# A two-layer attention and feed-forward kernel: first stack by groups of heads, empty products at the start, and row products with 72 columns of weights

## The chip, the cores and the metric

The kernel runs on one core of a Trainium2 chip. A core has a matrix engine (TensorE, here PE, whose weight loads are listed apart as PEld), a vector engine (VectorE, DVE), a scalar engine (ScalarE, ACT), a general engine (GpSimd, POOL), a queue engine (SyncE, SP) and sixteen DMA engines. Each engine works through its own instructions in the order in which they were written; between engines semaphores order the work. The metric is the time of one execution in microseconds on the device, as the median of several runs.

## The reference

The input is x of 8 batches x 512 tokens x 256 channels and a context of 8 x 512 x 128. Four blocks follow each other, each added to its input after a layer norm:

```python
x = x + L0_xattn(layernorm(x), ctx)   # causal self attention + cross attention, 16 heads of 16
x = x + L0_ffn(layernorm(x))          # quantised per token, 256 -> 1024 -> 256, gelu
x = x + L1_xattn(layernorm(x), ctx, ctx)  # cross attention, 16 heads of 16
x = x + L1_ffn(layernorm(x))          # quantised per tensor, 256 -> 1024 -> 256, gelu
# an attention: softmax(q @ k.T / 4) @ v for each head, then an output projection
# (for the self attention, keys after the query are masked)
```

All attention products are computed near single precision: a query or key is split into a high part and the rest, and the product of the two is taken as three terms.

## The kernel before

**Units, preps and groups.** An attention of one batch is a unit: S (causal self attention), C (cross attention of the first layer), X (cross attention of the second). There are 24 units. Each has 16 heads; a prep `n` covers the 8 heads of half a unit, and a group `G` covers 4 heads, as two pairs with one head in partitions 0 to 63 and one in 64 to 127. So unit 0 has preps 0 and 1, and groups 0 and 1 (of prep 0), 2 and 3 (of prep 1).

**What a prep does.** `ln_job` normalises x and turns it on TensorE into channels x tokens (`xlt`). `prep_job(n)` (line 550) multiplies it with the query and key weights, ScalarE adds the bias, and the result is split in a high and a low part (for preps 0 and 1 on VectorE, for all others on GpSimd). `stack_job(n)` (line 597) then copies by DMA, SBUF to SBUF, the parts into `qk_t`: 48 rows per head, three for each of 16 channels (high, low, high against high, high, low). It is six transfers of 256 KB, all issued from SP. Row 48 and 49 of a head carry the row maximum in two parts; the key side has ones there, written once by `init_job` (line 1361).

**What a group does.** `max_one` (line 668) multiplies queries with keys for a pair, both heads side by side in 64 rows of the array each, with 128 columns of weights; VectorE takes the negative maximum of each row into `mx`. For S units, mask products come first. `rows_job(n)` (line 706) waits for both groups of a prep, splits the maxima in two parts on GpSimd (`mhl`) and turns them into rows on TensorE: for each of 4 query tiles, and each half of 64 partitions, one product with 16 columns of weights and 64 moving columns. Two evacuations and two small transfers put the rows into `qk_t`. `exp_one` (line 756) then multiplies keys with queries over 50 rows, so that the maximum is already subtracted, and ScalarE takes the exponential into `p`. `av_part` (line 804) multiplies `p` with the values, four heads at a time in strips of 32 columns.

**What sets the order.** The whole program is laid out in Python before it runs. `Plan` (line 77) keeps a clock for each engine with modelled costs; `until(key)` lets a job wait until that event has a planned time. Each job is a generator, with a priority. The main loop (line 1452) picks, on TensorE's planned clock, the next maximum step, exponential step or value step, or lets a job run. Instructions land in each engine's queue in that order, and at run time each queue is in order. Thus SP issues transfers in planned order: one that waits for its data holds all behind it. `at["stack", G]` is the planned landing of the stack; V weights (`weights_job`), `init_job` and the next inputs (`inputs_jobs`) wait for `("stack", 0)`.

**The start.** SP issues x of batch 0 (512 KB, line 330), the first query and key weights (line 337), eight small transfers of biases (line 369), eight of identity and mask (line 374), and then the second halves of query and key weights (line 442). VectorE takes the batch-norm statistics and also reorders the columns of those four weights by small copies (line 449).

**Drains of the array.** The plan counts `SWITCH` when TensorE goes between products in 32-column strips over 128 rows ("cols") and products over 64 rows ("rows"); row products count as "rows", with `ROW_COLS` = 600 columns a block.

Of the kernel before, what the change touches and what calls it, by code (L numbers as in the profile page):

```python
# [17 lines left out]
P = 128  # L18
NT = T // P
# [57 lines left out]
class Plan:  # L77
# [43 lines left out]
    def dma(self, kb, *deps, dims=2, rate=195):  # L121
        t = self.run("sp", 0.33 if dims == 2 else 0.65, *deps)
        self.clock["dma"] = max(self.clock["dma"], t + 0.95) + kb / rate
        return self.clock["dma"] + 0.35
# [100 lines left out]
GQ, AHEAD = 4, 3  # L225
LINGER = 0.2
ROW_COLS = 600
DVE_HANDICAP = 0.8


# [56 lines left out]
def build(tc, A, out):  # L287
# [39 lines left out]


    first_x = tile("xa", [P, NT, C], F32, "xa_s0")
    nc.sync.dma_start(first_x, A["x"][0])  # L330
    at["x0"] = dma(512)
    heapq.heappop(plan.rings["xa"])
    first_raw = {}
    for i, nm in enumerate(("Sq", "Sk")):
# [16 lines left out]
    one = const.tile([P, 1], F32, name="one")  # L351
    nc.vector.memset(one, 1.0)
    ones_sq = one.broadcast_to([P, P])

    ident2 = const.tile([P, 2, P], BF16, name="ident2")
    mask2 = const.tile([P, 2, P], BF16, name="mask2")
# [75 lines left out]
    def weights_job():  # L432
        order = [(nm, u) for nm in ("Sq", "Sk", "Cq", "Ck", "Xq", "Xk") for u in range(2)]
        order[:4] = [("Sq", 0), ("Sk", 0), ("Sq", 1), ("Sk", 1)]
        for n, (nm, u) in enumerate(order):
            nk = WT[nm].shape[2]
            if n < 2:
                raw, t = first_raw[nm], at["raw", nm]
            else:
                yield from take("oc")  # L440
                raw = tile("oc", [P, T], F32, f"raw_{nm}{u}")
                nc.sync.dma_start(raw[:, : nk * P], WSRC[f"{nm}{u}"])
                t = dma(64 * nk)
            yield t + LAT
            for k in range(nk):
                for h in range(2):
                    full = raw[:, k * P : (k + 1) * P].rearrange("p (g c d h) -> p h c d g", g=2, c=2, h=2)
                    dst = WT[nm][:, u, k].rearrange("p (c d g h) -> p h c d g", c=2, g=2, h=2)
                    (nc.vector if n < 4 else nc.gpsimd).tensor_copy(dst[:, h], full[:, h])
                    t = plan.run("dve" if n < 4 else "pool", 0.2)  # L450
            give("oc", t)
            at["w", nm, u] = t
            if n == 3:
                yield from until(("stack", 0))
                for v in ("Vs", "Vc", "Vx", "Wp", "Wo"):
                    nc.sync.dma_start(WT[v].rearrange("p k m -> p (k m)"), WSRC[v])
                    at["w", v] = dma(256)
# [11 lines left out]
    def stats(x, nm):  # L469

        st = wp.tile([P, NT, 6], F32, tag="bnst", name=f"st_{nm}", bufs=3)
        mv = wp.tile([P, NT, 2], F32, tag="bnmv", name=f"mv_{nm}", bufs=3)
        r = wp.tile([P, NT], F32, tag="rstd", name=f"r_{nm}", bufs=3)
        neg = wp.tile([P, NT], F32, tag="nmean", name=f"nm_{nm}", bufs=3)
        for t in range(NT):
            nc.vector.bn_stats(st[:, t, :], x[:, t, :])
            op("dve", C)
            yield plan.now + 0.4
        for t in range(NT):
            nc.vector.bn_aggr(mv[:, t, :], st[:, t, :])  # L480
        te = plan.run("dve", 0.4)
        nc.gpsimd.tensor_scalar(r, mv[:, :, 1], LN_EPS, 0.0, ALU.add, ALU.add)
        nc.gpsimd.tensor_tensor(r, r, mhalf, ALU.pow)
        nc.gpsimd.tensor_scalar(neg, mv[:, :, 0], -1.0, 0.0, ALU.mult, ALU.add)
        te = plan.run("pool", 1.3, te)
        return mv[:, :, 1], neg, r, te
# [7 lines left out]
    def ln_job(key, src, nm, n_uses):  # L494

        if key[0] == "X":
            yield from until(("x3", key[1]))
        if key == ("S", 0):
            x = first_x
            yield at["x0"] + LAT  # L500
        else:
            yield from take("xa")
            x = tile("xa", [P, NT, C], F32, f"xa_{nm}")
            nc.sync.dma_start(x, src())
            yield dma(512) + LAT
        var, neg, r, te = yield from stats(x, nm)
        yield te
        for t in range(NT):
            if key == ("S", 0):
                at["first"] = nc.vector.tensor_scalar(  # L510
                    x[:, t, :], x[:, t, :], neg[:, t : t + 1], r[:, t : t + 1], ALU.add, ALU.mult
                ).ins.name
                te = op("dve2", C, te)
            else:
                te = normalise(x[:, t, :], x[:, t, :], neg, r, t)
        yield from take("xlt")
        xlt[key] = tile("xlt", [P, 2, T], F32, f"xlt_{nm}")
        uses[key] = [n_uses, 0.0]
        for k in range(2):
            yield pe_next(te)  # L520
            ps, pb = yield from gen_bank()
            for t in range(NT):
                wide(ps[:, t * P : (t + 1) * P], x[:, t, k * P : (k + 1) * P], ident)
            tm = plan.pe(4 * T, "cols")
            tm = evacuate(xlt[key][:, k, :], ps, T, tm)
            give_bank(pb, tm)
        give("xa", tm)
        at[key] = tm
# [21 lines left out]
    def prep_job(n):  # L550
# [26 lines left out]
        for i, (hi, lo) in enumerate(((0, 1), (3, 2))):  # L577
            wname, which = KIND[kind][i]
            key, ring = src_key(kind, b, which)
            yield from until(key, ("w", wname, u))  # L580
            xs = xlt[key]
            nk = xs.shape[1]
            ps, pb = yield from gen_bank()
            for k in range(nk):
                yield pe_next()
                wide(ps, WT[wname][:, u, k], xs[:, k, :], k == 0, k == nk - 1)
                tm = plan.pe(4 * T, "cols")
            used(key, ring, tm)
            ready.append((wname, ps, pb, tm, hi, lo))
            if n >= 2 or i == 1:  # L590
                for r in ready:
                    th = yield from split(*r)
                ready = []
# [3 lines left out]
    def stack_job(n):  # L597

        yield from until(("qkt", n))
        tf, tl = qkt_t.pop(n)  # L600
        if n >= NQK:
            yield from until(("exp", 2 * (n - NQK) + 1))
        dst = qk_t[n % NQK].bitcast(F32)
        for r, parts in enumerate((slice(0, 4, 3), slice(1, 4, 2), slice(0, 3, 2))):
            yield (at["qkt", n] if r < 2 else tl[1]) + LAT
            for c in range(2):
                nc.sync.dma_start(
                    dst[64 * c + r : 64 * c + 48 : 3].rearrange("p g w n -> p (g w n)"),
                    tf[64 * c : 64 * c + 64, parts, :],
                )  # L610
                t = dma(256, dims=3)
        at["stack", 2 * n] = at["stack", 2 * n + 1] = t
        give("qkt", t)

    VW = {"S": ("Vs", "S"), "C": ("Vc", "K"), "X": ("Vx", "K")}
# [87 lines left out]
        if s + 1 == len(MAX_STEPS) or MAX_STEPS[s + 1][0] != G:  # L703
            at["max", G] = t

    def rows_job(n):

        yield from until(("max", 2 * n), ("max", 2 * n + 1))
        m = mx_t.pop(n).rearrange("p c g t -> p t c g")
        hl = wp.tile([P, NT, 2, 2, 4], F32R, tag="mhl", name=f"mhl{n}", bufs=1)  # L710
        copy_ts(hl[:, :, :, 0], m)
        nc.gpsimd.tensor_tensor(hl[:, :, :, 1], m, hl[:, :, :, 0].bitcast(F32), ALU.subtract)
        t = plan.run("pool", 0.5)
        give("mx", t)
        yield pe_next(t)
        row = wp.tile([16, T], F32R, tag="mrow", name=f"mrow{n}", bufs=1)

        while (t := plan.bank_at("gn", 2)) is None:
            yield plan.now + 0.2
# [3 lines left out]
        for qt in range(NT):  # L723
            for h, i in enumerate(got):
                half = slice(64 * h, 64 * h + 64)
                nc.tensor.matmul(
                    banks[i][:16, qt * P :][:, half], hl[half, qt].rearrange("p c a g -> p (c a g)"), ident_r[half, half],
                    start=True, stop=True,
                )
        tm = plan.pe(ROW_COLS, "rows")  # L730
        t = 0.0
        for h, i in enumerate(got):
            dst, src = (
                x.rearrange("p (t n) -> p t n", t=NT)[:, :, 64 * h : 64 * h + 64] for x in (row, banks[i][:16])
            )
            te = evacuate(dst, src, T // 2, tm)
            give_bank(i, te)
            t = max(t, te)
        yield t + LAT
        for c in range(2):  # L740
            nc.sync.dma_start(
                qk_t[n % NQK].bitcast(F32)[64 * c + 48 : 64 * c + 50, :, 0], row.bitcast(F32)[8 * c : 8 * c + 8]
            )
            t = dma(16, dims=3)
        at["rows", 2 * n] = at["rows", 2 * n + 1] = t

    p_t, p_at, p_slots, av_t, scr_o = {}, {}, {}, {}, {}

# [610 lines left out]


    def init_job():
        yield from until(("stack", 0))
        yield from take("ev")
        ones = tile("ev", [4, T], F32, "ones_rows")

# [31 lines left out]
            if kind == "X":  # L1397
                yield from ln_job(("X", b), lambda b=b: x3_d[b], f"x{b}", 2)

    plan.start(series(rows_job(n) for n in range(2 * NU)), 0)  # L1400
    plan.start(series(evac_job(G) for G in range(NG - 2)), 0)
    plan.start(weights_job(), 0)
    plan.start(inputs_jobs(), 1)
# [370 lines left out]
```

## Time and profile before

| what | value |
|---|---|
| median of 3 runs | 1462.89 us (1462.37 to 1465.43) |
| the profiled execution | 1460.25 us, its span 1458.4 us |
| granted TensorE clock, mean | 0.971 |
| TensorE busy | 1374.8 us (94% of the span) |
| VectorE busy | 1142.0 us (78%) |
| ScalarE busy | 1035.5 us (71%) |
| GpSimd busy | 681.6 us (47%) |
| DMA queue of SP | 204.73 MB, 58.0% of 16 engines |
| row products, 64 rows x 16 columns, 64 moving | 384, in 48 blocks of 8 |

Page lines give busy time, share of the span and number of instructions of each engine, and then the span in 40 equal slices (36.5 us each): each digit is the busy share in tenths, and for PEclk the granted clock of TensorE in tenths of full speed. A timeline line has the start, the length, engine, source line, operation, output <- inputs, shapes and how many were merged; in brackets the idle time of the engine before it and what ended it. Nearly all operations carry the line of a helper (241 or 259), so tiles tell them apart: `pair<-qk` is a score product for maxima, `bank<-qk` one for exponentials, `bank<-ident_r,mhl` a row product, `bank<-p,v` a value product, `qk<-qkt` a stack transfer, `qk<-mrow` a transfer of rows. A busy PE counts from a product's start to its modelled end; consecutive products overlap, so steps between starts are read for rates.

### The profile page before, as it was taken

The page shows a single profiled execution, that of the slowest core. Times are in us where ns is not written, and L with a number is a line of the kernel's source. Part 1 is how long each engine was busy: PE and PEld are TensorE (multiplying, and loading weights), DVE is VectorE, ACT ScalarE, POOL GpSimd, SP SyncE. Part 2 cuts the span into 40 slices and gives each one's busy share as a digit, 9 for nine tenths or more (in the row PEclk, how much of TensorE's full clock was granted, in tenths as well). Part 3 has the DMA queues.
Part 4 walks back from the last instruction along what each step waited for, and adds up shares of the span by engine and source line. Part 5 has one row for each costly group of instructions (what it writes and reads, how often), then busy time and mean ns, then how long its engine had stood idle before and what let it go on. Part 6 is the DMA issues. An engine that isn't in the chain of part 4 may idle for free. (4 is left out here: it accounts for less than half of the span.)

```text
span 1458.4 us, 36089 instructions
## 1 busy us (share of the span) xinstructions
PE 1374.8 (94%) x14400; PEld 597.5 (41%) x14400; DVE 1142.0 (78%) x1591; ACT 1035.5 (71%) x1904; POOL 681.6 (47%) x1025
## 2 busy tenths in 40 slices
PE   4999999999999999999999999999999998999978
PEld 2443444444444444434344433443333333333527
DVE  4678588697788886898777996689899888766397
ACT  1456767677768867767677777668778795777587
POOL 1463355465455465464653552654455541524332
PEclk8899999999999999999899999999999999999899
DMA  6593565667576755665457655556647657373343
GB/s 126 152 216 76 133 139 125 142 138 182 132 161 150 161 129 141 156 161 126 105 126 155 163 126 132 142 120 160 163 105 169 155 149 196 105 176 110 117 142 116
DMA packets 155612, 207.03 MB, mean 142 GB/s; under 512 B 71940, under 2 KB 74244, under 8 KB 154932
## 3 DMA queue, kind: packets, MB, share of 16 engines
q1 hardware_dynamic: 155444, 204.73, 58.0%
q8 instruction: 113, 1.85, 0.5%
q14 instruction: 55, 0.45, 0.1%
HBM read 68.15 MB, written 47.43 MB: 79 GB/s over the span
## 5 line engine op out<-in xcount | busy, mean ns | idle before, releaser
L241 DVE TENSOR_REDUCE mx<-pair 128x2 f32<-128x1024 f32 (+3 forms) x768 | 808.9, 1086 | 210.7 <-PE pair L259 194.6
L241 ACT ACTIVATE p<-bank 128x512 f32<-128x512 f32 (+1 forms) x1408 | 712.0, 587 | 232.7 <-PE bank L259 224.8
L259 PE MATMUL bank<-p,v 128*32 128x512 f32 (+3 forms) x3072 | 371.7, 563 | 2.9 <-DVE mrow L241 1.3
L259 PE MATMUL bank<-qk 50*128 50x512 f32 (+3 forms) x1536 | 337.6, 433 | 16.2 <-ACT p L241 8.0
L259 PE MATMUL pair<-qk 48*128 48x512 f32 (+3 forms) x1536 | 325.5, 438 | 25.7 <-DVE mx L241 11.8
L259 PEld LDWEIGHTS bank<-qk 50*128 50x128 f32 x1536 | 159.6, 190 | 215.7 <-ACT p L241 142.9
L259 PEld LDWEIGHTS pair<-qk 48*128 48x128 f32 x1536 | 148.0, 191 | 171.5 <-DVE mx L241 83.4
L384 POOL TENSOR_SCALAR qkt<-qkt 128x512 fp32r<-128x512 f32 x92 | 57.1, 621 | 164.1 <-ACT qkt L241 157.5
L241 ACT ACTIVATE qkt<-bank,qk_bias 128x512 f32<-128x512 f32 x96 | 66.6, 693 | 81.0 <-PE bank L259 65.4
L409 POOL TENSOR_TENSOR qkt<-qkt 128x512 fp32r<-128x512 f32 x92 | 118.8, 1291 | 7.7
L259 PEld LDWEIGHTS bank<-p,v 128*32 128x32 f32 x3072 | 70.9, 109 | 114.6 <-issue 85.9
L384 POOL TENSOR_SCALAR mhl<-mx 128x32 fp32r<-128x32 f32 x48 | 11.8, 245 | 171.3 <-DVE mx L241 164.8
L883 POOL TENSOR_TENSOR yt<-oc,rb 128x512 f32<-128x512 f32 x31 | 39.8, 1283 | 73.3 <-DMA rb<-scrz 50.9
L259 PE MATMUL pair<-mask,ident 64*128 64x128 bf16 (+2 forms) x768 | 58.0, 226 | 6.9 <-DVE mx L241 4.7
L259 PE MATMUL bank<-ident,mask 64*128 64x64 bf16 (+1 forms) x768 | 52.7, 206 | 3.7 <-ACT p L241 1.2
L259 PEld LDWEIGHTS <-ident 64*128 64x128 bf16 x768 | 26.1, 97 | 71.0 <-issue 52.8
L259 PEld LDWEIGHTS <-mask 64*128 64x128 bf16 x768 | 25.8, 96 | 69.3 <-issue 61.0
L241 ACT COPY v<-bank 128x512 f32<-128x512 f32 x44 | 26.2, 596 | 39.4 <-PE bank L259 39.1
L241 ACT COPY ev<-bank 128x512 f32<-128x512 f32 x56 | 33.5, 598 | 17.9 <-PE bank L259 17.9
L241 DVE SCALAR_TENSOR_TENSOR h<-bank,so,bc_l_b 128x512 f32<-128x512 f32 x64 | 45.3, 741 | 0.9 <-PE bank L259 0.7
L241 ACT ACT_TABLE_LOAD x34 | 43.6, 1283 | 1.9 <-PEq L1762 0.7
L1189 POOL TENSOR_SCALAR h<-h,sh 128x1024 f32<-128x1024 f32 x32 | 36.0, 1125 | 17.7 <-DVE sh L241 15.2
(230 smaller groups left out, 1686.4 us busy)
## 6 DMA issues: line engine op xcount, KB each, us to landing
qk<-qkt SPq DMA_DIRECT2D x288, 256.0 KB
scro<-ev SPq DMA_DIRECT2D x94, 256.0 KB
oc<-scro SPq DMA_DIRECT2D x47, 256.0 KB
rb<-scrz SPq DMA_DIRECT2D x47, 256.0 KB
x_d<-xb SPq DMA_DIRECT2D x15, 512.0 KB
xa_s<-in_x SPq DMA_DIRECT2D x8, 512.0 KB
xb<-in_x SPq DMA_DIRECT2D x8, 512.0 KB
xr<-x_d SPq DMA_DIRECT2D x16, 256.0 KB
```

The costliest lines, as they stand in the source:

```text
L241: r = f(*args, **kw)
L259: r = self.eng.matmul(out, *args, **kw)
L384: nc.gpsimd.tensor_scalar(dst, src, 1.0, 0.0, ALU.mult, ALU.add)
L409: nc.gpsimd.tensor_tensor(dst, full, high.bitcast(F32), ALU.subtract)
L883: nc.gpsimd.tensor_tensor(y, o, rb, ALU.mult)
L1189: nc.gpsimd.tensor_scalar(ht, ht, s[:, t - t0 : t - t0 + 1], MAGIC, ALU.mult, ALU.add)
```

## The change

- x of batch 0 is loaded by two transfers of 256 KB.
- The column copies of the first query and key weights go to ScalarE; those of the second stay on VectorE.
- `keep_warm(n)` issues products of 128 rows, 128 columns and 512 moving columns of zeros into a bank pair that nothing reads: 8 at the start, 2 behind each of the four batch-norm statistics, 3 after them, and 16 behind prep 1's last projection.
- The stack of prep 0 is done by groups of heads: group 0's two pairs first, then group 1's, by 24 transfers of 64 KB, alternately from SP and ScalarE's queue. `at["stack", 0]` and `at["stack", 1]` are now two events; V weights and the rows of ones wait for the second, the next inputs for the first.
- For prep 0 a row job runs for each group by itself; all other preps are as before.
- A row product takes 72 columns of weights (`WIDE`): its 16 (or 8) columns and whatever lies behind them in a tile that is cleared once. The additional output rows are not read.

```diff
+WIDE = 72
...
-    nc.sync.dma_start(first_x, A["x"][0])
-    at["x0"] = dma(512)
+    for t in range(0, NT, 2):
+        nc.sync.dma_start(first_x[:, t : t + 2], A["x"][0][:, t : t + 2])
+        at["x0", t] = dma(256)
...
+    zero_b = zero.bitcast(BF16)[:, 0:1]
+
+    def keep_warm(n, behind=None):
+
+        for _ in range(n):
+            r = nc.tensor.matmul(
+                pairs[3][:, 0], zero_b.broadcast_to([P, P]), zero_b.broadcast_to([P, T]), start=True, stop=True
+            )
+            if behind is not None:
+                tc.add_manual_dep(r.ins, behind.ins.name, SYNC, reason="warm")
+                behind = None
+
+    keep_warm(8)
...
-                    (nc.vector if n < 4 else nc.gpsimd).tensor_copy(dst[:, h], full[:, h])
-                    t = plan.run("dve" if n < 4 else "pool", 0.2)
+                    if n < 2:
+                        nc.scalar.copy(dst[:, h], full[:, h])
+                    else:
+                        (nc.vector if n < 4 else nc.gpsimd).tensor_copy(dst[:, h], full[:, h])
+                    t = plan.run("act" if n < 2 else "dve" if n < 4 else "pool", 0.2)
...
             if n == 3:
-                yield from until(("stack", 0))
+                yield from until(("stack", 1))
...
-            nc.vector.bn_stats(st[:, t, :], x[:, t, :])
+            r_st = nc.vector.bn_stats(st[:, t, :], x[:, t, :])
+            if nm == "s0":
+                keep_warm(2, r_st)
...
+        if nm == "s0":
+            keep_warm(3, r_st)
...
-            yield at["x0"] + LAT
+            yield at["x0", 0] + LAT
...
+            if (n, i) == (1, 1):
+                keep_warm(16)
...
+        rows = (slice(0, 4, 3), slice(1, 4, 2), slice(0, 3, 2))
+
+        for g in range(2 if n == 0 else 0):
+            for r, parts in enumerate(rows):
+                yield (at["qkt", n] if r < 2 else tl[1]) + LAT
+                for pair in (2 * g, 2 * g + 1):
+                    for c, q in enumerate((nc.sync, nc.scalar)):
+                        q.dma_start(
+                            dst[64 * c + r : 64 * c + 48 : 3, pair], tf[64 * c + pair : 64 * c + 64 : 4, parts, :]
+                        )
+                    plan.run("act", 0.65)
+                    t = dma(128, dims=3)
+            at["stack", g] = t
+        for r, parts in enumerate(rows if n else ()):
...
-        at["stack", 2 * n] = at["stack", 2 * n + 1] = t
+        if n:
+            at["stack", 2 * n] = at["stack", 2 * n + 1] = t
...
+    hl_t = wp.tile([P, 48 + WIDE], F32R, name="mhl")
+    nc.gpsimd.memset(hl_t.bitcast(F32), 0.0)
+
+    def rows_job(n, g0, ng):
+
+        yield from until(*(("max", 2 * n + g) for g in range(g0, g0 + ng)))
+        last = g0 + ng == 2
+        ps = slice(2 * g0, 2 * (g0 + ng))
+        m = mx_t[n].rearrange("p c g t -> p t c g")[:, :, :, ps]
+        k = 8 * ng
+        hl = hl_t[:, : NT * k].rearrange("p (t c a g) -> p t c a g", t=NT, c=2, a=2)
...
-                    banks[i][:16, qt * P :][:, half], hl[half, qt].rearrange("p c a g -> p (c a g)"), ident_r[half, half],
+                    banks[i][:WIDE, qt * P :][:, half], hl_t[half, qt * k : qt * k + WIDE], ident_r[half, half],
...
-        at["rows", 2 * n] = at["rows", 2 * n + 1] = t
+        for g in range(g0, g0 + ng):
+            at["rows", 2 * n + g] = t
...
     def init_job():
-        yield from until(("stack", 0))
+        yield from until(("stack", 1))
...
-    plan.start(series(rows_job(n) for n in range(2 * NU)), 0)
+    rows = [(0, 0, 1), (0, 1, 1)] + [(n, 0, 2) for n in range(1, 2 * NU)]
+    plan.start(series(rows_job(*r) for r in rows), 0)
```

## The prediction

> **What bounds the kernel now.** I read the page first: engines, then slices.
>
> ```profile
> PE 1374.8 (94%) x14400; PEld 597.5 (41%) x14400; DVE 1142.0 (78%) x1591; ACT 1035.5 (71%) x1904; POOL 681.6 (47%) x1025
> ...
> PE   4999999999999999999999999999999998999978
> ...
> PEclk8899999999999999999899999999999999999899
> ```
>
> TensorE bounds everything but the first slice (36 us, PE 4 tenths) and the tail. So the change has two prices: what the start gives back, and what a longer row product adds in the middle. The tail's chain (27 us of DVE gmax, 26 us of output products) isn't touched.
>
> Next the timeline of the first 60 us (start, length, instruction, idle before it and its releaser).
>
> ```profile
> 12.40 0.53 SPq L442 DMA_DIRECT2D raw_Sq<-in_wa  x1
> ...
> 14.74 0.54 DVE L241 COPY w_Sq<-raw_Sq 128x64 f32<-128x64 f32 x4 [4.66 <-DMA raw_Sq<-in_wa]
> ...
> 15.63 0.42 DVE L241 CAST qkt<-qkt 128x512 fp32r<-128x512 f32 x1
> ...
> 17.49 9.00 SPq L607 DMA_DIRECT2D qk<-qkt  x12
> ...
> 18.03 0.69 ACT L241 ACTIVATE qkt<-bank,qk_bias 128x512 f32<-128x512 f32 x1 [1.03 <-PE bank L259]
> ...
> 27.27 0.47 PE L259 MATMUL pair<-qk 48*128 48x128 f32 x1 [7.31 <-DMA qk<-qkt]
> ...
> 45.31 0.24 POOL L384 TENSOR_SCALAR mhl<-mx 128x32 fp32r<-128x32 f32 x1 [31.84 <-DVE mx L241]
> ...
> 56.89 2.06 ACT L241 ACTIVATE p<-bank 128x512 f32<-128x512 f32 x4 [2.75 <-PE bank L259]
> ```
>
> The stack (twelve transfers of 256 KB for preps 0 and 1) is issued from 17.49; scores begin at 27.27, when the first six have landed. Both groups' maxima end at 45.3 (POOL takes them up), and the first exponential runs at 56.89. The same stretch by windows (length, busy PE, PEld, DVE, ACT, POOL, granted clock, DMA share, GB/s):
>
> ```profile
> 20.00:27.00 7.00, 0.00 (x0) 0.00 (x0) 1.12 (x2) 0.43 (x1) 0.00 (x0) 0.70 1.08 192
> 27.00:34.00 7.00, 4.81 (x36) 3.79 (x36) 3.98 (x7) 0.00 (x0) 0.00 (x0) 0.50 1.08 190
> 34.00:44.00 10.00, 9.35 (x82) 4.89 (x82) 7.17 (x10) 0.42 (x1) 0.00 (x0) 0.54 0.89 268
> ...
> 120.00:1340.00 1220.00, 1175.42 (x12696) 492.20 (x12692) 985.57 (x1348) 898.56 (x1706) 592.25 (x883) 0.98 0.60 142
> ```
>
> To be seen: the stack runs at 190 GB/s with the DMA full, PE idles 7 us, then works at half clock until 43; in the middle PE is busy 96%.
>
> Last, a row product between scores (PE timeline, near 1222 us), and the loads of a 128-column score pair:
>
> ```profile
> 1221.84 0.49 PE L259 MATMUL pair<-qk 48*128 48x512 f32 x2
> 1222.17 0.29 PE L259 MATMUL bank<-ident_r,mhl 64*16 64x64 f32 x8
> 1222.32 0.50 PE L259 MATMUL pair<-qk 48*128 48x512 f32 x2
> ```
>
> ```profile
> 45.53 0.31 PEld L259 LDWEIGHTS pair<-qk 48*128 48x128 f32 x4
> ```
>
> **The front end (x halves, copies on ACT, warm-up).** x landed at 4.37. In halves, the first about 1 us earlier; without the eight weight copies (2 x 0.52) between its instructions DVE ends the statistics at about 5.5, not 6.9, and normalising starts near 7.3, not 8.7. Nineteen empty products of 512 columns, at 0.215 us warm (the tail's 512-column products step by that) or 0.43 at half clock, take 4 to 8 us of a PE with nothing to do before 9.16; transposes that took 3.59 should come near twice 1.07, the warm pair at 65 and 67 us. So the first projections end some 2.5 us earlier. I cost this at **nothing**, because of a queue: SP issues without a pause to 13.4, and the second pair of raw weights is issued at 12.40, behind sixteen small transfers of 0.6 each. The extra x half moves it to 12.84. Its copies stay on DVE, and in the order written out they precede the splits (planned about 9 us, the splits after 12). So DVE splits from 15.63 + 0.44 = 16.07, then by rows 0.45 + 0.69 + 0.43: first stack issue at about **17.65**, 0.15 later than before. What the cover is worth if gone: 2.5 us.
>
> **The stack in groups.** Prep 0 becomes 24 transfers of 64 KB, half from ACT. Group 0 is 12: six per queue at about 0.7 (SP's twelve took 9.0) end at 21.9; its 786 KB at 190 GB/s need 4.1, so issue and data agree on landing near **23.4**, against 27.27: -3.9. Group 1 lands near 27.5. The Trainium skill speaks against the second queue ("DMA: Bandwidth & Descriptors", Issuing engines are not separate DMA queues): transfers from several engines run on the same DMA engines, and only issue time is saved. The row says when that matters: at 256 KB the rate bound it (1.38 us of data per 0.75 of issue); at 64 KB the data take 0.34 and one queue's issue 0.7. From one queue group 0 would land at 28, by two at 23.4; I take the row.
>
> What stands behind ACT's twelve issues: prep 1's two evacuations, 18.03 and 19.75 before. They wait until 17.65 + 12 x 0.67 = 25.7; DVE's splits follow, and prep 1's stack is issued near 28. Context and next x (768 KB; the plan releases them at group 0's landing) now go ahead of it. Its 1.57 MB land near 39 instead of 35. Needed then? Before, the second prep's maxima began only at 44.9.
>
> **Array warm at the scores.** Sixteen empty products follow prep 1's last projection, which the second raw weights still hold to about 19.6: 3.4 us, to 23.0, just before the stack lands. They delay nothing unless the stack comes earlier. Then DVE sets the pace: the sixteen maxima of both groups are 3.08 + 6.35 + 2.00 + 1.23 = 12.7 us of DVE, stretched to 17.9 at half clock. From 23.4 they end near 37, not 45.3: -8. Group 0's rows are ready near 31. First exponentials still need the rows of ones (issued 37.4 to 41.6 before, now behind prep 1's stack) and their own small transfer: about 46, not 56.9: -10.9. Meanwhile V, the next transposes and the next query projection fill PE. Prep 2 moves too: its key weights were issued at 49.71 behind a row transfer on which SP had stood 4.7 us. So between 8 and 11; since maxima lead by less, I take **-9**. Ends: 0 if something late takes it back, -13 if prep 2 comes 10 us earlier as well.
>
> **The row products.** 48 blocks of 4 x 2, 16 columns wide, become 49 (the extra one in the DVE-bound start, with two POOL operations, two evacuations, two 8 KB transfers: hidden). The two halves run side by side; pairs step by 0.03 us, 64 columns streamed. A 72-column load is longer than that. The row: a 128-column pair of the same type steps 0.31 - 0.19 = 0.12. The skill ("TensorE: Matmul & The Clock Gate", LDWEIGHTS) has columns / 1.2 in ns: 107 at 128, where the row agrees, and an estimate of 60 at 72, where no row is. Three steps: +0.09. After a product in 32-column strips the first load isn't hidden: +0.05 more. I counted 21 blocks behind scores or masks, 27 behind others: 21 x 0.09 + 27 x 0.14 = **5.7 us of PE**.
>
> And what is saved? The skill ("TensorEngine Tiling (Array Packing)", Key Properties) says that a change of tiling mode drains the array; 16 columns are another mode than 128. Of the blocks' 96 borders 41 are to scores or masks. The drain that the trace shows, between 128-row and 64-row products, is 0.095 (512-column strip products step 0.427, to a score 0.522). By the rule 41 x 0.095 = 3.9 saved, net +1.8. The row: a score at 1221.84, a load of 0.11 and 0.21 of streaming end at 1222.16; the product starts at 1222.17. After it a score follows in 0.15, and at 941.82 within 0.03 of the last product. There is no drain to save; I take the row. Some added time falls into PE's waits (4% of the middle), so of 5.7 I count **+3.5**; ends -1 and +5.7.
>
> **Sum.** -9 + 3.5 = -5.5. The profiled execution took 1460.25 (span 1458.4, 1.85 around it), 2.6 below the median of 1462.89; on the median: **1457.4**. A planner orders everything from one clock, so a moved start shuffles all later queues; I allow 3 us either way.
>
> **Rivals.**
> - Slower: *prep 1's stack late behind ACT's queue.* For: twelve issues precede two evacuations, and two loads go ahead of its six transfers. Each microsecond past 39 is taken from the start; at 45 to 46 nothing is left, since maxima of prep 1 began at 44.9. An issue on ACT of 1.0, as SP's longest here (1.01), adds 4; loads of V weights (1.3 MB) slipped ahead add 3.5 to 7. Then only the row loads remain: 1462.9 + 3.5 = **1466.4**. Against: 6 us of slack.
> - *The division does pay*: a cost of 16 columns that single starts don't show, or loads hidden. Rows cost 0 or -1: **1453**.
> - *The array isn't warm*: score products with gaps may not hold the clock; at half clock the maxima take 17.9 again. Only -3.9 remains, plus 3.5: **1462.5**. For: 27 to 43 stayed at half clock though PE worked.
>
> **How the numbers follow.** As worked out 0.45 (1454 to 1461), division pays 0.17, late stack 0.28, array cold 0.10. A measurement of this kernel tells about 0.2% (2.9 us) from no change. Faster: the first two, 0.62; same: mainly the cold array, 0.10; slower: 0.28. The range leaves out the outer part of the first and last: 1450 to 1468; the likeliest's own is 1454 to 1461.
>
> **What would show it.** First stack issue at 17.5 to 17.8 (at 15: the front end counted after all); first score at 23 to 24; clock full from about 20; maxima of group 1 done near 37; first exponential near 46; ACT evacuating prep 1 near 26; prep 1's maxima by 40. In the middle: 72-column pairs stepping 0.06, not 0.03, and the same 0.02 at borders to scores. I am wrong if first exponentials stay near 56, or if the blocks take no longer than before.

## The result and the profile after

The changed kernel takes 1479.26 us, median of 4 runs (1476.72 to 1482.22), against 1462.63 us of the kernel before in the same set (4 runs). The ratio is 1.0109, 95% interval 1.0077 to 1.014. The forecast was 1457.4, range 1450 to 1468. It is **slower by 16.6 us** where 5.5 us of gain were expected. The profiled execution took 1476.72 (span 1474.9).

The page of the kernel after: engines, then the row of TensorE's busy tenths and the row of its granted clock.

```profile
PE 1387.3 (94%) x14436; PEld 605.6 (41%) x14443; DVE 1139.3 (77%) x1583; ACT 1040.2 (71%) x1914; POOL 679.5 (46%) x1028
...
PE   7999999999999999999999999999999999999978
...
PEclk9989999999999999999989999989999999899999
```

TensorE is busy 12.5 us more than the 1374.8 shown of before, and its first slice has gone from 4 tenths to 7. Some of that is the empty products. The timeline of the first 62 us (start, length, instruction, the idle before it and what ended that):

```profile
13.39 0.53 SPq L457 DMA_DIRECT2D raw_Sq<-in_wa  x1
...
15.75 0.53 DVE L242 COPY w_Sq<-raw_Sq 128x64 f32<-128x64 f32 x4 [7.44 <-DMA raw_Sq<-in_wa]
...
16.64 0.43 DVE L242 CAST qkt<-qkt 128x512 fp32r<-128x512 f32 x1
...
18.16 7.74 SPq L635 DMA_DIRECT2D qk<-qkt  x12
18.16 8.07 ACTq L242 DMA_DIRECT2D qk<-qkt  x12
...
23.55 0.88 PE L260 MATMUL pair<-qk 48*128 48x128 f32 x4
...
26.28 1.26 ACT L242 ACTIVATE qkt<-bank,qk_bias 128x512 f32<-128x512 f32 x2 [12.37 <-PE pair L260]
...
34.22 5.05 SPq L644 DMA_DIRECT2D qk<-qkt  x6
...
43.77 0.21 POOL L399 TENSOR_SCALAR mhl<-mx 128x16 fp32r<-128x16 f32 x1
...
47.86 4.03 ACT L242 ACTIVATE p<-bank 128x512 f32<-128x512 f32 x8 [0.59 <-PE bank L260]
```

This is nearly the start that was forecast. DVE waits for the second raw weights (13.39), the stack of prep 0 is issued at 18.16 on both queues, the first score runs at 23.55, where it was 27.27, and the first exponential at 47.86, where it was 56.89: 9 us earlier. Two steps are late: prep 1's stack is issued at 34.22, and GpSimd takes up group 1's maxima at 43.77 (DVE ends them at 42.76). By windows (length, busy PE, PEld, DVE, ACT, POOL, granted clock, DMA share, GB/s):

```profile
20.00:27.00 7.00, 5.41 (x37) 2.86 (x36) 2.49 (x5) 0.72 (x2) 0.00 (x0) 1.00 0.56 201
27.00:34.00 7.00, 4.05 (x34) 2.90 (x34) 6.50 (x11) 0.54 (x1) 0.44 (x2) 0.63 0.87 298
34.00:44.00 10.00, 10.00 (x146) 4.81 (x148) 6.81 (x14) 2.82 (x6) 6.20 (x16) 0.92 0.89 170
120.00:1340.00 1220.00, 1169.56 (x12546) 493.11 (x12543) 970.73 (x1331) 888.44 (x1684) 575.52 (x857) 0.97 0.61 140
```

The clock is full when the scores start, falls to 0.63 between 27 and 34, and is 0.92 in the next ten microseconds. In the middle TensorE is busy 1169.56 of 1220 us, where it was 1175.42. So the start was won, and yet the end is late. The windows of the first 130 us say where the head start went. The kernel after:

```profile
0.00:60.00 60.00, 50.12 (x616) 26.16 (x617) 32.25 (x76) 22.38 (x50) 17.59 (x47) 0.94 0.57 165
60.00:130.00 70.00, 61.48 (x578) 24.61 (x578) 52.43 (x68) 32.03 (x64) 41.74 (x62) 0.88 0.58 129
```

and the kernel before:

```profile
0.00:60.00 60.00, 39.33 (x434) 22.00 (x436) 35.77 (x83) 11.07 (x19) 13.72 (x34) 0.80 0.58 140
60.00:130.00 70.00, 68.31 (x728) 28.47 (x726) 50.67 (x71) 41.72 (x88) 44.14 (x71) 0.95 0.62 150
```

In the first 60 us the changed kernel starts 616 products, 34 of them empty, against 434. From 60 to 130 us it starts 578 against 728. After 130 us both stand at almost the same count (1160 useful ones against 1162): a head start of some 150 products is gone, and the clock of the second window is 0.88 where it was 0.95. The timeline of that stretch in the kernel after:

```profile
48.22 2.00 SPq L1112 DMA_DIRECT2D bc_l_b<-in_l_b  x2
...
50.27 0.43 SPq L1282 DMA_DIRECT2D l0w1f<-in_l_w  x1
...
51.13 0.33 SPq L457 DMA_DIRECT2D raw_Ck<-in_wb  x1
...
59.56 0.46 POOL L467 COPY w_Ck<-raw_Ck 128x64 f32<-128x64 f32 x2 [1.53 <-DMA raw_Ck<-in_wb]
```

```profile
65.33 0.62 POOL L399 TENSOR_SCALAR qkt<-qkt 128x512 fp32r<-128x512 f32 x1
...
65.97 5.41 SPq L644 DMA_DIRECT2D qk<-qkt  x6
...
76.44 0.79 PE L260 MATMUL pair<-qk 48*128 48x512 f32 x1 [5.14 <-DMA qk<-qkt]
```

Prep 2's first key weights leave SP at 51.13, behind two bias rows and the 1 MB of the FFN's first weights. GpSimd's copy waits for them to land and starts at 59.56, 8.4 us after the issue. ACT has evacuated the projection at 61.98, but GpSimd first works off what stands ahead in its queue, the normalising of the next input and two copies of weights; it splits prep 2 at 65.33, and SP issues its stack at 65.97. TensorE, which has by then used up all that preps 0 and 1 gave, stands 5.14 us for it. From 73.1 to 83.4 the granted clock is half. In the kernel before, split and stack were at the same times, and prep 2's first score 2.7 us later:

```profile
42.57 0.43 SPq L1232 DMA_DIRECT2D l0w1f<-in_l_w  x1
...
49.71 12.23 SPq L442 DMA_DIRECT2D raw_Ck<-in_wb  x2
...
61.53 0.48 POOL L449 COPY w_Ck<-raw_Ck 128x64 f32<-128x64 f32 x2
...
65.49 0.62 POOL L384 TENSOR_SCALAR qkt<-qkt 128x512 fp32r<-128x512 f32 x1 [1.58 <-ACT qkt L241]
...
66.14 3.72 SPq L607 DMA_DIRECT2D qk<-qkt  x4
...
79.16 0.50 PE L259 MATMUL pair<-qk 48*128 48x512 f32 x1
```

There the FFN's weights were issued 7 us ahead of the first keys (the second line merges two issues, at 49.71 and 61.62), and GpSimd copied the keys only behind the normalising of the next input, which ran from 54.88 to 60.77. So the scores of prep 0 and the first exponentials moved 2 to 9 us forward, prep 1's maxima began 1.7 us later (47.27, before 45.61), and prep 2's stack didn't move: by chance two different waits put it at the same time in both kernels.

### The profile page after: what moved, and what is told of

The parts are those of the page before. It is cut to its first block, busy times and chain, and to the rows that moved or that the text cites. A ratio compares the mean times of both kernels' runs of the same rounds, so it can differ in the third digit from the quotient of the medians.

```text
span 1474.9 us, 36213 instructions
## 1 busy us (share of the span) xinstructions
PE 1387.3 (94%) x14436; PEld 605.6 (41%) x14443; DVE 1139.3 (77%) x1583; ACT 1040.2 (71%) x1914; POOL 679.5 (46%) x1028
## 3 DMA queue, kind: packets, MB, share of 16 engines
q1 hardware_dynamic: 155304, 203.95, 58.5%
## 5 line engine op out<-in xcount | busy, mean ns | idle before, releaser
L399 POOL TENSOR_SCALAR mhl<-mx 128x32 fp32r<-128x32 f32 (+1 forms) x49 | 11.8, 241 | 166.5 <-DVE mx L242 160.2
L242 ACT CAST mrow<-bank 16x256 fp32r<-16x256 f32 (+1 forms) x83 | 25.8, 354 | 20.0 <-PE bank L260 19.7
```

The costliest lines, as they stand in the source:

```text
L242: r = f(*args, **kw)
L399: nc.gpsimd.tensor_scalar(dst, src, 1.0, 0.0, ALU.mult, ALU.add)
```

## The experiments

All times are medians; the kernel before, run beside them, gave 1462.75 (17 runs), 1462.91 (37) and 1463.23 (19) in the three sets. Each ratio is to the runs of its own set.

**Row products of 72 columns alone.** The kernel before, with only the operand made wider, out of a tile that is cleared once as in the change (those lines are left out here):

```diff
-                    banks[i][:16, qt * P :][:, half], hl[half, qt].rearrange("p c a g -> p (c a g)"), ident_r[half, half],
+                    banks[i][:WIDE, qt * P :][:, half], hl_t[half, qt * 16 : qt * 16 + WIDE], ident_r[half, half],
```

> The kernel before, with one thing of the change: row products of 72 columns. Order of every queue as before. If row loads cost what the products' own steps in the changed kernel show (0.11 more inside a block, 0.05 more in front of it for 27 of 48 blocks, some of it absorbed), 1465 to 1469, +2 to +6. If they are the main cause of the loss, 1473 to 1479. If dividing the array as the scores do pays after all, below 1462.

Measured: 1472.29 (4 runs, 1471.94 to 1473.81), ratio 1.0067 (1.0052 to 1.0082), so **+9.5 us**. A block of row products between scores in this kernel, near 1233 us:

```profile
1233.48 0.50 PE L260 MATMUL pair<-qk 48*128 48x512 f32 x2
1233.58 0.50 PEld L260 LDWEIGHTS bank<-ident_r,mhl 64*72 64x72 f32 x8
1233.81 0.39 PE L260 MATMUL bank<-ident_r,mhl 64*72 64x64 f32 x8
```

The first row product starts 0.33 us after the second score, as it did with 16 columns (1221.84 and 1222.17 of before). The block itself is 0.39 long where it was 0.29. Laid block against block on the two traces, from the first start to the start of the next other product, a block takes 0.10 us more in the median where it follows a score or mask, 0.145 more after a strip product. Two blocks that fell into half clock took 0.38 and 0.37 more, and five that hold a wait of their own took 0.03 or less. All 48 make 5.8 us. The rest comes in steps where windows of half clock fall in other places.

**The start alone.** The changed kernel with 16 columns in place of 72:

```diff
-WIDE = 72
+WIDE = 16
```

> The changed kernel with 16 columns in the row products, so the start's parts alone; order of every queue as in the changed kernel. If the start itself loses (its head start is gone when prep 2's stack comes, and the new order after it is worse), 1472 to 1476, +9 to +13. If the row loads are the main cause, 1458 to 1466.

Measured: 1471.57 (6 runs, 1467.72 to 1476.36), ratio 1.0061 (1.004 to 1.0081): **+8.8 us**. So each half of the change loses by itself, and 9.5 + 8.8 = 18.3 is near the 16.6 of both. The row products are not what ate the head start.

**The start without empty products.** The same, without the 35 empty products:

```diff
-    keep_warm(8)
...
-            if nm == "s0":
-                keep_warm(2, r_st)
...
-        if nm == "s0":
-            keep_warm(3, r_st)
...
-            if (n, i) == (1, 1):
-                keep_warm(16)
```

> As the start alone with 16 columns, and without the 35 empty products; the order of all other instructions stays. If the warm array is worth what the first maxima gain by it, first exponentials 3 to 6 us later, but the end within 2 us of the run with empties, because prep 2's stack takes the head start away in either case. If warmth carries to the end, 4 us or more slower than with empties.

Measured: 1472.33 (12 runs, 1465.4 to 1483.28), ratio 1.0068 (1.0045 to 1.0091), within the scatter of the run above. The profile fell on the longest of these runs, so its later lines aren't compared; at its start the array was at half clock from 23 to 40 us. The warm array is worth nothing measurable at the end here, while prep 2 is late. It is tried again below, with prep 2 in time.

**Prep 2's key weights first.** The start with 16 columns, and one line that lets SP load prep 2's keys ahead of the query weights of prep 3:

```diff
         order[:4] = [("Sq", 0), ("Sk", 0), ("Sq", 1), ("Sk", 1)]
+        order[4:8] = [("Cq", 0), ("Ck", 0), ("Cq", 1), ("Ck", 1)]
```

> The changed start with row products of 16 columns, and prep 2's key weights loaded ahead of the second half of its query weights (Cq0, Ck0, Cq1, Ck1). If the head start of 9 us is lost because prep 2's key weights land behind 1.5 MB of FFN weights (51.1 us, its stack issued at 66 as before the change), the stack of prep 2 is now issued before 60 us, TensorE no longer waits 5 us near 71 to 76, and the time is 1456 to 1464. If the shifted order of the planner after the start is what costs, it stays at 1468 to 1474.

Measured: 1463.8 (18 runs, 1458.62 to 1471.59), ratio 1.0007 (0.9991 to 1.0022). That is **7.8 us** less than the start without this line: nearly all of its loss. The timeline:

```profile
41.22 0.39 SPq L458 DMA_DIRECT2D raw_Ck<-in_wb  x1
...
48.52 0.46 POOL L468 COPY w_Ck<-raw_Ck 128x64 f32<-128x64 f32 x2
...
52.35 0.43 SPq L1283 DMA_DIRECT2D l0w1f<-in_l_w  x1
...
53.22 0.34 SPq L458 DMA_DIRECT2D raw_Cq<-in_wa  x1
...
53.68 5.51 SPq L645 DMA_DIRECT2D qk<-qkt  x6
```

The keys leave at 41.22 and the stack at 53.68; in the start without this line it was 53.17 and 67.19. No wait of 5 us is left (the longest of TensorE from 60 to 130 us is 1.7), and the windows show it:

```profile
0.00:60.00 60.00, 50.57 (x591) 24.83 (x591) 30.70 (x74) 20.99 (x46) 19.89 (x48) 0.89 0.53 155
60.00:130.00 70.00, 66.59 (x712) 29.07 (x704) 64.79 (x85) 39.19 (x81) 39.20 (x63) 1.00 0.60 142
```

There are 712 products in the second window at full clock, where the start without this line had 597 at 0.88.

**The same order in the kernel before**, as a control (the same line added to it):

> The kernel before with the same order of prep 2's weights alone, as a control. If that order is worth something only together with the earlier start, the time is within 3 us of 1462.7. If it is good by itself, it is below 1459.

Measured: 1461.59 (20 runs, 1451.94 to 1467.29), ratio 0.9992 (0.9975 to 1.001): no difference at the end. In its profile the early keys do win 3 to 5 us up to 224 us (the maxima of the table below end at 78.4, 127.5 and 219.2), and by 278 us nothing of that is left.

**Row products of 128 columns alone**, to tell the length of a weights load from the division of the array, which 72 and 128 columns share (`WIDE = 128` in the first experiment):

> The kernel before with row products of 128 columns in place of 16. If the length of the weights load sets their price, a block of eight takes 0.25 to 0.30 us more and the 48 blocks 12 to 13 us, with what the clock adds 1475 to 1480 (against 1472.3 with 72 columns). If only the mode of the array decides, it is 1462 to 1466 or as with 72 columns.

Measured: 1479.5 (4 runs, 1469.82 to 1489.15), ratio 1.0133 (1.0072 to 1.0193). A block between scores:

```profile
1231.41 0.50 PE L260 MATMUL pair<-qk 48*128 48x512 f32 x2
1231.52 0.65 PEld L260 LDWEIGHTS bank<-ident_r,mhl 64*128 64x128 f32 x8
1231.75 0.53 PE L260 MATMUL bank<-ident_r,mhl 64*128 64x64 f32 x8
```

Of 0.29, 0.39 and 0.53 us at 16, 72 and 128 columns nothing is a step at a change of the division: the block grows with the load, and the first product still starts 0.34 after the score. Blocks take 0.24 more than before after a score, 0.33 after a strip product (medians); all 48 make 12.8 us. The rest of the 16.6 is uncertain, since the interval is 10.5 to 28 us wide.

**Keys first, no empty products.** The fourth experiment without the 35 empties:

> The changed start with row products of 16 columns and prep 2's keys loaded first (1463.8), without the 35 empty products. If the empty products carry part of what the mended start wins (the half clock windows fall to 13.7 us before 80 us from 27.3), the time rises to 1466 to 1469. If the warm array is worth nothing at the end, as it was while prep 2 was late, it is 1461 to 1465.

Measured: 1462.12 (10 runs, 1457.82 to 1466.56), ratio 0.9996 (0.9969 to 1.0022). Without the empties it is, if anything, shorter than with them (1463.8). The warm array brings nothing measurable even where prep 2 is in time. And this is the fastest form of the new start, with no measurable gain over the kernel before.

**The whole change with the keys first**:

> The whole change, row products of 72 columns included, with prep 2's key weights loaded ahead of the second half of its query weights. If the late keys and the wider row products are separate prices, this is the changed kernel's 1479.3 less 8, about 1471.5 (1469 to 1474). If they are one and the same loss, it is near 1464 or stays near 1479.

Measured: 1470.73 (10 runs, 1463.76 to 1479.33), ratio 1.0051 (1.0028 to 1.0074). The one line takes 8.5 us off the changed kernel, as it took 7.8 off its start alone; 6.9 us stay over the same kernel with 16 columns. So the two prices are separate.

**The FFN's weights later**, in the start with 16 columns, the order of prep 2's weights as it was:

```diff
     def ffn0_weights_job():
-        yield from until(("stack", 3))
+        yield from until(("stack", 5))
```

> The changed start with row products of 16 columns and the old order of prep 2's weights; instead the FFN's weights (1.5 MB and their row sums) wait for prep 4's stack in place of prep 2's neighbour. If it is the FFN's transfers ahead of prep 2's keys in SP's queue that lose the head start, the time falls from 1471.6 to 1462 to 1466, as with the keys first. If the cause is the serial chain of weight copies on GpSimd, it stays at 1469 to 1473.

Measured: 1490.74 (4 runs, 1489.39 to 1500.96), ratio 1.0211 (1.0162 to 1.0261). Both expectations missed. The edit moved the FFN's whole work and with it the plan of the rest, so the total says nothing about the start. Its trace does, up to some 220 us. In this table a point of progress is the end of a given one of the 768 row maxima on DVE, in us, with the difference to before:

```
maximum no.     before   changed   start, 16   + keys first   + no empties   FFN later
    33            81.6     -2.2       -1.3         -8.9          -10.4         -7.5
    65           130.4     +0.6       +1.7         -9.9          -10.5         -4.5
   129           224.1     +0.2       +0.8         -9.3           -9.8         -5.2
   161           278.0     +5.0       +5.1         -4.7           -4.7         +0.3
   273           462.7     +9.3       +7.2         -0.6           -2.2         +3.6
   481           833.6    +11.7       +5.2         -0.8           +0.3        +16.5
   753          1311.7    +18.4      +12.5         +6.0           +6.0        +28.9
```

With the FFN's transfers out of the way prep 2's stack is issued at 61.45 rather than 67.19, and 4.5 to 7.5 us of the head start are there up to 224 us. The keys-first order had brought the stack 13.5 us forward; so the FFN's transfers account for 5.7 of these, and the rest would belong to the keys' place in the chain of weight copies, which this edit left alone.

The reordered line also changes what the planner lays out later. But the two starts, with and without it, are 7.6 us apart at maximum 33, where prep 2 begins, and 11.6 at 65; 6.5 of that are left at 753. The gap arises at prep 2 and not in the later order.

## Why the prediction was wrong

**Front end at nothing: right.** DVE waited 7.44 us for the second raw weights, which left SP at 13.39, not 12.84; the first stack was issued at 18.16 where 17.65 was forecast. The idle work ahead of it bought nothing.

**The stack in groups: right for group 0, right in its place and wrong in its size for prep 1.** The first score came at 23.55 (23.4 forecast), and ACT evacuated prep 1 at 26.28 (25.7). But prep 1's stack went out at 34.22, not 28. The five V weights and six transfers of ones, 27.05 to 34.1, stood ahead of it on SP: the forecast of the late-stack rival had named V weights as the thing that could slip ahead, and the sum of the likeliest case left them out. The maxima of prep 1, forecast by 40, began at 47.27. No wait for the stack is in the trace, as it had landed by then.

**Array warm: half right.** The clock was full from 20 to 28.8 and half from there to 35.6, where the scores, paced by DVE, left gaps, as the rival of a cold array had it. Group 1's maxima ended at 42.76, not 37 (45.22 before). The forecast stretched only the maxima themselves. DVE also had prep 1's splits, 2.2 us from 27.00 on, and 1.9 us of the next input's statistics between them, and TensorE took 4.7 us of V products between the scores. And two experiments show that the empty products bring nothing measurable (third and seventh).

**First exponential near 46: nearly right** (47.86, 9 us earlier).

**"Prep 2 moves too ... I take -9": the step that failed.** I had read that the key weights of prep 2 were issued at 49.71, behind a row transfer on which SP stood, and took it that an earlier row transfer would let them go earlier. The row transfers moved (39.37 and 46.43, where the one of before was at 48.30), and the keys left later than before. The plan takes the weights one after another, each when GpSimd has copied the last, and the FFN's weights, released by prep 1's stack, went directly ahead of the keys: 51.13. From there to the stack (65.97) it is 15 us, 8.4 of them until the keys have landed and 3.4 in GpSimd's queue, and this chain wasn't followed in the forecast. So the head start ended at prep 2: 5.1 us of wait until 76.4, and half clock on to 83.4, which is 3.4 us of work lost; half clock from 117.5 for 6.8 us takes as much again, where it was 3.4 us long before. Measured term: **+8.8 instead of -9**. Of these 17.8 us, 7.8 are shown to be the late keys by one reordered line. The other 10 are a head start that is there until 225 us and then goes; that cause stays open.

**What isn't settled.** With the keys early, 9 to 10 us of head start are there until 225 us, and at the end of the kernel none is left. The trace shows places, not a cause: 4.6 us go at 237 us, where a row product waits 2.5 us for a bank that ACT frees and half clock lasts 6.8; 4 us by 463, with half clock at 378 and at 456; 4 us at 938 to 948 (below). In sum 15.3 us go between maxima 129 and 753 (224 and 1312 us). By the two traces 6.8 of them are more idle time of TensorE, and about 8.5 are the half that 17.1 us more of half clock lose.

Part of that is likely the draw of one profile. From 237 to 256 us all ten other profiles have half clock for 3.4 to 6.8 us, those with the queues of before and wider row products among them; only the profile of before has none. Nor do the profiles show that a warmer start is paid back later: half clock from 270 us on was 55.3 us before, 67.2 with the keys first, but 58.5 without the empties and 52.0 in the whole change with the keys first. Over all runs the mean granted clock with the keys first was the higher one (0.9714 in 18 runs, 0.9691 in 37 of before). Why TensorE idles more, no run here shows. Runs of the kernel before alone lie between 1454.8 and 1474.1.

**The row products: the price of a block was right, the sum wasn't.** Forecast were 0.09 and 0.14 a block; measured 0.10 and 0.145. In part that is luck: behind a score the first of the three steps stayed at 0.033, so the steps gave 0.06, and 0.04 came behind the last product. No drain was there to save: with 16, 72 and 128 columns the first row product starts 0.33 to 0.34 after the score ahead of it, as the row had it and not the rule of the Trainium skill ("TensorEngine Tiling (Array Packing)", Key Properties) as the forecast applied it. The term that was mis-sized is "of 5.7 I count +3.5". TensorE's waits absorbed hardly anything (5.8 are in the trace), and the measured price of the whole is **+9.5**. The difference seems to be the clock: a new half clock window at 249.5 us costs 1.7, and one of 13.7 us near 1246, where it was 10.2, costs 1.9. Over the 37 runs of the kernel before in one set, time goes up by 1.0 us for each 0.001 that the mean granted clock is lower (correlation -0.88); the four runs with 72 columns have a mean of 0.9668, the 17 of before in their set 0.9694, which would make 2.6 us. With four runs that is an argument and not a proof. "The division does pay" falls.

The rival that ended slower, 1466.4, named another place (prep 1's stack) for what happened one prep later.

## What to carry to other kernels

A head start is worth what the first thing that doesn't move lets through. Follow the moved work to its next input, that input's transfers, and their place in the queue and in the chain of small copies behind them, before counting it; here one prep further was enough.

In this kernel, where TensorE is busy 94% of the span, microseconds added to it came out whole, and more: 5.8 us of longer blocks cost 9.5, and 12.8 cost 16.6. Little idle time stood ready to absorb them.

## What the runs showed of the hardware

**Short waits close the clock.** The times in the clock records lie multiples of 3.413 us apart. I divided the eleven profiles of this study on that grid, from 100 us on, and took TensorE's idle share in each full-clock window. After windows idle for half or more, half clock followed 54 times in 68; for 30 to 50% idle, 45 in 122; for 20 to 30%, 15 in 149; for less, 13 in 3834. No window ahead of half clock had more than 2.93 us idle, the median had 1.6. Half clock lasted 3.4 to 13.7 us, 5.9 in the mean; half of that is lost, so by estimate a wait of 1 to 2 us that closes the clock costs about 3 us more. Ends of products are modelled, so the shares are near values. The Trainium skill ("TensorE: Matmul & The Clock Gate", HAM oscillation — how this bites in real kernels) warns of gaps over about 3.4 us; here gaps well below that did it. One such place, in the keys-first kernel:

```profile
938.01 0.40 PE L260 MATMUL pair<-qk 48*128 48x512 f32 x1
...
940.44 0.48 PE L260 MATMUL pair<-qk 48*128 48x512 f32 x1 [2.04 <-DMA qk<-qkt]
...
941.63 1.93 PE L260 MATMUL bank<-xlt_x,w_Xq 128*32 128x512 f32 x8
```

and its windows, on the grid:

```profile
934.00:937.40 3.40, 3.40 (x54) 1.57 (x52) 0.10 (x1) 3.40 (x9) 3.31 (x6) 1.00 1.08 197
937.40:940.80 3.40, 1.36 (x16) 0.73 (x14) 0.00 (x0) 1.75 (x4) 1.95 (x5) 0.99 1.28 154
940.80:947.60 6.80, 6.80 (x41) 2.16 (x43) 2.94 (x3) 2.40 (x5) 0.37 (x1) 0.50 0.63 230
947.60:951.00 3.40, 3.40 (x56) 1.37 (x51) 3.40 (x5) 0.00 (x0) 1.52 (x2) 1.00 0.03 5
```

The score waits 2.04 us for its stack, 60% of that window is idle, and the next 6.8 us are granted 0.50: eight 512-column products take 1.93, where at full clock they take 1.07. The kernel before, over the same times:

```profile
937.40:940.80 3.40, 2.97 (x36) 1.44 (x32) 0.42 (x1) 2.81 (x7) 3.01 (x6) 1.00 0.95 190
940.80:947.60 6.80, 6.80 (x86) 2.47 (x84) 5.87 (x7) 2.34 (x5) 1.90 (x2) 1.00 0.70 237
```

It waited 0.43 us at this product, and the clock stayed full. If the share of a window is what counts, the same wait can close the clock or not, as it falls into one window of the grid or across two; the grid lies differently in each profile. That would fit the 1% by which runs of one kernel differ, but no run here shifted the grid alone.

**Weights loads.** Where nothing else waits, the second and third step between pairs of row products took 0.030 to 0.035 us at 16 columns, 0.062 to 0.065 at 72 and 0.109 to 0.112 at 128 (medians of all blocks). The Trainium skill ("TensorE: Matmul & The Clock Gate", LDWEIGHTS) has columns / 1.2 in ns for a load, which makes an estimate of 0.060 at 72 and 0.107 at 128: these traces agree. The first step stays at 0.033 behind a score at either width; behind a strip product it took 0.086 and 0.133, so there the load lengthens the first step too.
